# Eight tiles to a group in a fused quantised-FFN, attention and FP6 kernel: one chain of numbers per eight tiles, long stages by four

## The chip, the cores and the metric

The kernel runs on one core of a Trainium2 chip. The metric is device time in microseconds (us) of one execution, the median over runs. The compute engines are TensorE (PE, with its weight loads as PEld), VectorE (DVE), ScalarE (ACT) and GpSimd (POOL); SyncE (SP) issues all the kernel's DMAs from one queue, in order.

## The reference

`x` is [128, 64, 256] float32: 128 sequences of 64 tokens; `cond` is [128, 256]. In short, `x = x + ffn(recurrence(cond, x))`, and the output is `x + fp6_linear(block(x, cond))`. The four parts are:

1. A gated recurrence over the 64 steps, from `cond` as the first `h` and with `x` as `z`: `h = tanh(h * leak + sigmoid(h @ Wh.T + z @ Wz.T + b) * z)`.
2. A SwiGLU feed-forward (256 to 704 to 256) with int8 fake quantisation of activations and weights. The scales are maxima over the whole tensor, so `h` must be known everywhere before the down projection.
3. A hyperbolic transformer block, conditioned by `ada = t_emb @ w_ada + b_ada` (shift, scale and gate, twice). `logmap0` and `expmap0` scale every token by a function of its norm:

```
xm  = expmap0(layer_norm(logmap0(x)) * (1 + sc_msa) + sh_msa)
... attention over 64 tokens with 16 heads of 16, output projection
x   = mobius_add(x, expmap0(g_msa * logmap0(attn_out)))
xm  = expmap0(layer_norm(logmap0(x)) * (1 + sc_mlp) + sh_mlp)
ff  = plin(plin(xm, w_f1, b_f1), w_f2, b_f2)
x   = mobius_add(x, expmap0(g_mlp * logmap0(ff)))
```

4. A linear layer (256 to 256) on activations and weights rounded to an FP6 grid with a scale per 32 values.

`mobius_add(x, y)` needs, for each token, the sums x.x, y.y and x.y; everything else in it is arithmetic on these numbers. That arithmetic, and that of logmap0, expmap0 and layer_norm, is what "number chains" means below.

## The kernel before

**Up to about 310 us** the recurrence runs (PE, ACT and DVE in turn), then the first feed-forward products are made and `h` is written to DRAM (`h_d`). The change does not touch this.

**`fused`** does the rest over 64 tiles of 128 tokens. A group has GT = 4 tiles, so there are 16 groups; the work is done in pairs of tiles. Its stages:

- `front(i)`: loads `h` (`hl`, two pairs ahead) and `x` (`xr`), quantises to int8 on POOL, casts (`hq`), does the down projection on PE (`dn`), writes the block input `x1` to SBUF and to DRAM (`x1_d`), and takes mean and variance of every token (`stats`).
- `norms(k)`: `ln_coeffs`, a chain of some 22 small DVE steps with two reciprocal roots, for attention's group k + LA and mlp's group k together, with one column for each tile (2 x GT columns). Then `modulate` (scale and shift by `ada` rows, with the sum of squares `un`), `radial` (the root of `un`, `su`) and `clip_ball`.
- `attention(i)`: qkv in three passes of split float32, head norms, scores, softmax, values; then `radial` of `tn` (`full`), the output projection `wo`, the gate (POOL multiply, L737) and two sums of squares (`tail_sums`).
- `mlp(i)`: the product of both linear layers as one, `radial` of `fn2` (`cf`), gate, sums, and x.(ga) by `x_dot`.
- `tail(k)`: for the attention result it loads `x1` again from DRAM (`xt`) and takes x.(ga) by `x_dot`; then `tail_coeffs`, a chain of some 30 small DVE steps, for attention's group k and mlp's group k - LM together; then `combine` (L797, one DVE step a tile) for both, and `stats` of attention's result.
- `fp6(i)`: block maxima, scaling, rounding, transposes, the last linear layer (`fp`), the addition of `x1` read from DRAM, and the store.

The program order is a loop over k that calls tail(k), norms(k), fp6(k - LM), mlp(k), attention(k + LA), front(k + LA + 1), with LA = 5 and LM = 3. This is not the order on the engines: the framework's scheduler (`schedule_with_timeline_sim=True`) places instructions on each engine by a simulated time, and functions marked `@first` (`radial`, `ln_coeffs`, `tail_coeffs`) have a raised priority. Once built, every engine and the SP queue run their lists strictly in order. CFG holds the buffer counts of each pool tag and which engine (V, G, S) does which step.

Reciprocal roots are made by `rsqrt` in one of two ways: as a power on POOL (L640) if there are at most `len_pow` = 16 columns, otherwise by ln and exp on ACT (L643, L644) and a Newton step of three DVE instructions (L645 to L647).

Of the kernel before, what the change touches and what calls it, by code (L numbers as in the profile page):

```python
# [16 lines left out]
AF = mybir.ActivationFunctionType  # L17
# [5 lines left out]
P = 128  # L23
# [21 lines left out]
TS = 4  # L45
CFG = {'rnd': 'S', 'ef': 8, 'fill': {'x1a': 'V', 'mod0': 'V'}, 'hold': [3, 0], 'mk': 3, 'mv': 6, 'xs': 3, 'la': 3, 'sb': 7, 'qks': 'GGGG', 'deq': 'VV', 'first': 1000, 'hb': 2, 'q_h': 'P', 'q_x1': 'P', 'q_xr': 'P', 'q_ot': 'P', 'q_out': 'P', 'q_ada': 'P', 'room': [[0.3, 0.3, 0.55], [0.5, 0.4, 0.2]], 'qv': 64, 'p1': 'GVGVGVGV', 'x1': 3, 'u1': 16, 'u2': 6, 'qkv': 2, 'sq': 1, 'uT1': 2, 'uT2': 2, 'qM': 2, 'kT': 2, 'e': 4, 'oT': 1, 'yT': 1, 'hq': 2, 'hl': 2, 'xr': 1, 'ot': 2, 'ada00': 2, 'ada02': 2, 'ada10': 2, 'ada12': 4, 'dn': 1, 'qk': 2, 'sc': 2, 'ao': 1, 'ml': 1, 'fp': 1, 'mod0': 'GGGV', 'mod1': 'VVVV', 'sqm0': 'SSSS', 'sqm1': 'SSSS', 'su0': 'VVVV', 'su1': 'VGVG', 'q8': 'GGGGGG', 'hqc': 'SSSVVV', 'qm': 'SSSS', 'x1a': 'GV', 'gate0': 'GGGG', 'gate1': 'GGGG', 'yb': 'GG', 'va': 'GGGG', 'sqt': 'SSSS', 'sqg': 'SSSS', 'sqo': 'SSVS', 'f2e': 'SSSS', 'early': 0, 'q8f': 'VVVVVV', 'hqf': 'SSSVVV', 'fl': 1, 'un': 2, 'jsu': 1, 'LA': 5, 'LM': 3, 'tl': 6, 'ord': 1, 'xt': 3, 'q_xt': 'P'}
GT = 4
NGR = NTILE // GT

# [501 lines left out]
def fused(ctx, tc, a, out_tok, x_tok, L):  # L551
# [13 lines left out]
    one = ones[:, 0:1]  # L565
    len_pow = 4 * GT
    nhalf = ep.tile([P, len_pow], F32, name="nhalf", tag="nhalf", bufs=1)
# [15 lines left out]
    class Pairs:  # L583


        def __init__(self, tag):
            self.t = [big(tag, [P, 2, D]) for _ in range(GT // 2)]

# [124 lines left out]

    def modulate(src, nm, aa, which, i0, u, un):

        for g in range(GT):
            ss = load_ada(which, 0, 2, i0 + g)
            ug = u[g]
            if pick(f"mod{which}", g) == "G":
                G_.tensor_scalar(ug, src[g], nm[:, g : g + 1], aa[:, g : g + 1], ALU.add, ALU.mult)  # L720
                G_.tensor_tensor(ug, ug, ss[:, 1, :], ALU.mult)
                G_.tensor_tensor(ug, ug, ss[:, 0, :], ALU.add)
            else:
                V.scalar_tensor_tensor(ug, src[g], nm[:, g : g + 1], ss[:, 1, :], ALU.add, ALU.mult)  # L724
                V.scalar_tensor_tensor(ug, ug, aa[:, g : g + 1], ss[:, 0, :], ALU.mult, ALU.add)
            square_sum(pick(f"sqm{which}", g), f"u{which}", ug, un[:, g : g + 1])

    def clip_ball(u, su, which):

        for g in range(GT):  # L730
            scale(pick(f"su{which}", g), u[g], u[g], su[:, g : g + 1])

# [91 lines left out]

    pairs = range(GT // 2)

# [24 lines left out]

    def front(i):

        i0 = at[0] = i * GT
        x1 = x1s[i] = Pairs("x1")
        mv1 = get_mv(i - LA)[:, HA, :]
        for h2 in pairs:
            pr = i0 // 2 + h2
# [28 lines left out]

    def attention(i, u, sums):

        i0 = at[0] = i * GT  # L890
        oall = u
        tn = mk("tn", GT)
        for h2 in pairs:
            qkv = big("qkv", [P, 2, 3 * D])
# [96 lines left out]
            for g in (2 * h2, 2 * h2 + 1):  # L991
                square_sum(pick("sqo", g), "o", oall[g], tn[:, g : g + 1])
        full = radial(tn, "full", R, 1.0 / RATIO)
        av = u
        for h2 in pairs:
            pt = bank("ao")
            for i in range(2):
                for c in range(2):
                    o = (2 * i + c) * P
                    turn(pt[:, o : o + P], oall[2 * h2 + i][:, c * P : (c + 1) * P])  # L1000
            oT = big("oT", [P, 4, P])
            S.copy(oT.rearrange("p c t -> p (c t)"), pt)
            pm = bank("ao")
            for i in range(2):
                g = 2 * h2 + i
                for c in range(2):
                    PE.matmul(pm[:, i * D : (i + 1) * D], lhsT=oT[:, 2 * i + c, :], rhs=wo[:, c, :],
                              start=(c == 0), stop=(c == 1))
            for i in range(2):
                g = 2 * h2 + i  # L1010
                V.scalar_tensor_tensor(av[g], pm[:, i * D : (i + 1) * D], full[:, g : g + 1], bo,
                                       ALU.mult, ALU.add)
                gb = load_ada(0, 2, 1, i0 + g)
                tail_sums(av[g], gb[:, 0, :], sums, g, 0, "a")
        return av

    def mlp(i, u, x2, sums):

        i0 = at[0] = i * GT
        fn2 = mk("fn2", GT)  # L1020
        for h2 in pairs:
            uT = big("uT2", [P, 2, 2, 2 * P], F32R)
# [7 lines left out]
            for i in range(2):  # L1030
# [9 lines left out]
                V.tensor_tensor_reduce(out=junk3, in0=pm[:, :D], in1=u[g], scale=1.0, scalar=0.0,  # L1040
                                       op0=ALU.mult, op1=ALU.add, accum_out=fn2[:, g : g + 1])
                if pick("f2e", g) == "S":
# [4 lines left out]
        av = u  # L1047
        for g in range(GT):
            V.scalar_tensor_tensor(av[g], u[g], cf[:, g : g + 1], bf2,  # L1049
                                   ALU.mult, ALU.add)  # L1050
# [5 lines left out]
    def fp6(i, av, s2):  # L1056

        i0 = at[0] = i * GT
        sab = mk("sab", GT)
        S.activation(sab, s2, AF.Abs)  # L1060
        for h2 in pairs:
            y = av.t[h2].rearrange("p g d -> p (g d)")
# [4 lines left out]
            hh = slice(2 * h2, 2 * h2 + 2)  # L1067
            V.scalar_tensor_tensor(of(msc), of(msc), 1.0 / 7.5, bc_in(sab[:, hh], 8), ALU.mult, ALU.mult)
            V.tensor_scalar(msc, msc, 1e-30, None, ALU.max)
# [27 lines left out]
    def norms(k, xs):  # L1097

        on_a, on_m = k + LA < NGR, k >= 0
        mv = mvs.pop(k)  # L1100
        un, nm = mk("un"), mk("nm")
        if not (on_a and on_m):
            G_.memset(un, 1.0)
        x2n, la = ln_coeffs(mv, xs)
        V.tensor_scalar(nm, mv[:, :, 0], -1.0, None, ALU.mult)
        todo = []
        if on_m:
            um = ums[k] = Pairs("u2")
            todo.append((1, k, us[k], um, HM))
        if on_a:  # L1110
            ua = uas[k + LA] = Pairs("u1")
            todo.append((0, k + LA, x1s[k + LA], ua, HA))
        for which, i, x, u, h in todo:
            at[0] = i * GT
            modulate(x, nm[:, h], la[:, h], which, i * GT, u, un[:, h])
            if not CFG["jsu"]:
                clip_ball(u, radial(un[:, h], f"su{which}"), which)
        if CFG["jsu"]:
            su = radial(un, "su")
            for which, i, x, u, h in todo:  # L1120
                clip_ball(u, su[:, h], which)
        if on_a:
            G_.tensor_copy(get_tail(k + LA)[2][:, HA], x2n[:, HA])
        if on_m:
            G_.tensor_copy(get_tail(k + LM)[2][:, HM], x2n[:, HM])

    def tail(k):
# [3 lines left out]
        if on_a:  # L1131

            own = mk("xss", bufs=CFG["sb"])
            G_.memset(own, 1.0)
            x1 = Pairs("xt")
            for h2 in pairs:
                move("xt", out=x1.t[h2], in_=x1_d[:, GT * k + 2 * h2 : GT * k + 2 * h2 + 2, :])
            for g in range(GT):
                x_dot(x1[g], uas[k][g], sums(k, HA), g, "a")
        ag2, xg, x2n = tails.pop(k)  # L1140
        s_, r = tail_coeffs(ag2, xg, x2n, xss.pop(k - LM, None), own, HA, HM)
        if on_a:
            u, mv = uas.pop(k), get_mv(k)

            for g in range(GT):
                combine(u[g], x1[g], u[g], r[:, HA], g)
                stats(mv[:, HM, :][:, g, :], u[g], 2)
# [11 lines left out]
    for i in range(CFG["fl"]):  # L1159
        front(i)  # L1160
    for k in range(-LA, NGR + LM):
        done = tail(k) if k >= 0 else None
        if done and CFG["ord"] == 0:
            fp6(k - LM, *done)
        if k < NGR:
            norms(k, xss.get(k))
        if done and CFG["ord"] == 1:
            fp6(k - LM, *done)
        if 0 <= k < NGR:
            mlp(k, ums[k], us[k], sums(k + LM, HM))  # L1170
        if k + LA < NGR:
            attention(k + LA, uas[k + LA], sums(k + LA, HA))
        if done and CFG["ord"] == 2:
            fp6(k - LM, *done)
        if k + LA + CFG["fl"] < NGR:
            front(k + LA + CFG["fl"])

# [47 lines left out]
```

## Time and profile before

| | |
|---|---|
| median of 13 runs | 1382.49 us (1376.08 to 1390.08) |
| the profiled execution | 1380.64 us, span 1378.7 us |
| DVE busy | 1150.2 us, 83%, 3608 instructions |
| PE busy | 1088.3 us, 79% |
| POOL busy | 828.2 us, 60% |
| ACT busy | 813.8 us, 59% |
| mean granted TensorE clock | 0.862 |
| bytes read from HBM, written | 115.94 MB, 46.14 MB |

Busy times are from one profiled execution. Rows of the profile name the line, the engine, the operation and out<-in by the program's names; after the first bar stand the busy time in us and the mean ns of one, after the second the engine's idle time before them and what ended it. A row of the stretch view has for each engine its busy us with the count of instructions, then the mean granted TensorE clock, the DMA share and GB/s. A row of the waits view has the total us, the number of times and the longest.

### The profile page before, as it was taken

The numbers are of one execution on the slowest core, as the hardware profiler recorded it, in microseconds if no ns is written. First come the engines' busy times: TensorE is split into PE (matmuls) and PEld (weight loads), VectorE is DVE, ScalarE is ACT, GpSimd is POOL, SyncE is SP. The second block draws the span as 40 slices with busy tenths as digits, with TensorE's granted clock in tenths as the row PEclk, the third lists the DMA queues.
The fourth block names the chain that finished last, engine by engine and source line by source line (L and its number), as shares of the span: only waits on it lengthen the run. The fifth ranks groups of instructions, "written<-read, shape, count | busy, mean of one in ns | idle before, by whom it ended". The sixth has DMA issues, their size and how long they took to land. (4 is left out here: it accounts for less than half of the span.)

```text
span 1378.7 us, 23854 instructions
## 1 busy us (share of the span) xinstructions
PE 1088.3 (79%) x7364; PEld 740.7 (54%) x7380; DVE 1150.2 (83%) x3608; ACT 813.8 (59%) x2364; POOL 828.2 (60%) x1043
## 2 busy tenths in 40 slices
PE   7999967974489887898868888598987889785645
PEld 4656542332366555666646666466655666553433
DVE  5666669996888788998998879999799998889873
ACT  2545438981376756667746667555766676744341
POOL 3111208865588867787775776768667675746551
PEclk9999979995699978999858999788998899886575
DMA  7112245669724414442154441504414131314211
GB/s 235 54 54 85 70 194 194 267 256 286 225 88 124 123 49 141 136 150 68 51 172 125 131 132 44 160 26 136 139 39 138 55 112 50 104 58 121 62 47 46
DMA packets 119305, 163.65 MB, mean 119 GB/s; under 512 B 10885, under 2 KB 72074, under 8 KB 119178
## 3 DMA queue, kind: packets, MB, share of 16 engines
q1 hardware_dynamic: 119178, 162.13, 37.7%
q8 instruction: 58, 0.95, 0.3%
q14 instruction: 69, 0.57, 0.1%
HBM read 115.94 MB, written 46.14 MB: 118 GB/s over the span
## 5 line engine op out<-in xcount | busy, mean ns | idle before, releaser
L609 ACT ACTIVATE junk<-u 128x256 bf16<-128x256 f32 x432 | 183.0, 426 | 149.6 <-POOL u L737 53.8
L915 PE MATMUL qk<-wqkv,uT 128*128 128x512 f32 (+1 forms) x768 | 183.8, 377 | 15.8 <-DVE uT L906 9.5
L737 POOL TENSOR_TENSOR u<-u,ada 128x256 f32<-128x256 f32 x128 | 101.7, 797 | 101.8 <-ACT junk L609 95.0
L915 PEld LDWEIGHTS qk<-wqkv,uT 128*128 128x128 f32 x768 | 126.8, 201 | 37.2 <-DVE uT L906 13.2
L981 PE MATMUL ao<-va,e 128*64 128x34 f32 x2048 | 91.3, 246 | 62.5 <-DVE u L986 22.8
L981 PEld LDWEIGHTS ao<-va,e 128*64 128x64 f32 x2048 | 82.1, 161 | 88.9 <-issue 49.6
L966 PE MATMUL sc<-qM,kT 64*64 64x256 f32 x1024 | 122.9, 425 | 5.0 <-ACT kT L956 3.4
L1037 PE MATMUL ml<-wm,uT 128*128 128x512 f32 (+1 forms) x384 | 115.0, 437 | 0.0
L1037 PEld LDWEIGHTS ml<-wm,uT 128*128 128x128 f32 x384 | 80.3, 211 | 52.1 <-issue 22.0
L616 ACT ACTIVATE qM<-sc,mhead 128x256 f32<-128x256 f32 x256 | 102.0, 494 | 5.8 <-PE sc L92 5.7
L945 POOL TENSOR_TENSOR va<-qkv,comb 64x256 f32<-64x256 f32 x128 | 85.1, 665 | 32.2 <-PE ao L981 26.2
L880 PE MATMUL dn<-wdT,hq 128*128 128x256 bf16 (+1 forms) x384 | 67.8, 321 | 45.7 <-DVE x L882 20.6
L513 POOL TENSOR_TENSOR hv<-uv,sil 128x512 f32<-128x512 f32 x44 | 57.6, 1312 | 66.3 <-DVE am L516 48.5
L974 ACT ACTIVATE e<-sc 128x512 f32<-128x512 f32 x128 | 72.5, 599 | 28.9 <-PE ao L981 15.2
L609 ACT ACTIVATION_READ_ACCUMULATOR junk<-u 128x1 f32 x432 | 86.9, 201 | 0.0
L434 PE MATMUL pg<-hsT,WT 128*128 128x128 f32 x504 | 75.8, 290 | 9.5 <-ACT hsT L446 9.0
L1091 PE MATMUL fp<-wfT,yT 128*128 128x256 f32 x256 | 83.2, 458 | 0.0
L434 PEld LDWEIGHTS pg<-hsT,WT 128*128 128x128 f32 x504 | 65.1, 192 | 31.5 <-ACT hsT L446 28.8
L941 POOL TENSOR_TENSOR qkv<-qkv,comb 128x512 f32<-128x512 f32 x64 | 69.6, 1103 | 16.8 <-DVE comb L932 5.7
L620 POOL TENSOR_SCALAR hb<-hl,cu 128x1280 int8<-128x1280 f32 x64 | 62.9, 988 | 26.8 <-DMA hl<-h_d 11.5
L966 PEld LDWEIGHTS sc<-qM,kT 64*64 64x64 f32 x1024 | 54.7, 143 | 43.1 <-issue 10.2
L880 PEld LDWEIGHTS <-hq 128*128 128x128 bf16 (+1 forms) x384 | 38.1, 110 | 72.5 <-issue 33.7
(285 smaller groups left out, 3162.6 us busy)
## 6 DMA issues: line engine op xcount, KB each, us to landing
ada<-ada_d SPq DMA_DIRECT2D x128, 256.0 KB, 3.6
h_d<-hv SPq DMA_DIRECT2D x80, 256.0 KB, 2.1
hl<-h_d SPq DMA_DIRECT2D x32, 640.0 KB, 5.9
ada<-ada_d SPq DMA_DIRECT2D x128, 128.0 KB, 2.5
xt<-in_xT_dram SPq DMA_DIRECT2D x16, 512.0 KB, 4.7
xr<-in_x_dram SPq DMA_DIRECT2D x32, 256.0 KB, 3.8
x_d<-x SPq DMA_DIRECT2D x32, 256.0 KB, 2.3
xt<-x_d SPq DMA_DIRECT2D x32, 256.0 KB, 2.9
```

The source lines that it names most:

```text
L434: lp = PE.matmul(pg[c][:, st], lhsT=WT[:, k, c * P : (c + 1) * P], rhs=hp[:, k, :], start=False, stop=False, skip_group_check=True)
L609: S.activation(junk, src, AF.Square, accum_out=acc)
L616: S.activation(dst, src, AF.Copy, scale=by)
L737: ENG[pick(f"gate{which}", g)].tensor_tensor(av, av, gb, ALU.mult)
L880: PE.matmul(py[:, i * D : (i + 1) * D], lhsT=hq[r, j, i * P : (i + 1) * P], rhs=wdT[r, j, :], start=(i == 0 and j == 0), stop=(j == 5), sk ...
L915: PE.matmul(pm[:, :n_], lhsT=uT[:, z, k, cs], rhs=wqkv[:, w, k, lo:hi], start=False, stop=(k == 1 and q == 2))
L945: ENG[pick("va", g)].tensor_tensor(va[r, :, s, 0:HD], qkv[r, xy, 512:768].rearrange("p (h d) -> p h d", d=HD), bc_in(comb[r, xy * 48 + 32 ...
L966: PE.matmul(sc[rr][s * T : (s + 1) * T, c * 256 : (c + 1) * 256].rearrange("p (v t) -> p v t", v=4), lhsT=kTs[xy][r, c, s * T : (s + 1) * ...
L974: S.activation(e.rearrange("p c v t -> p (c v t)"), sc[rr], AF.Exp, scale=1.0 / math.sqrt(HD))
L981: PE.matmul(pv[xy * T : (xy + 1) * T, hh], lhsT=E[2 * xy + hh // 4][:, c, hh % 4, :], rhs=vas[(2 * h2 + xy) % 4][:, c * 8 + hh], start=Tru ...
L1037: PE.matmul(pm[:, cs], lhsT=uT[:, z, k, i * P : (i + 1) * P], rhs=wm[:, w, k, cs], start=False, stop=(k == 1 and q == 2))
L1091: PE.matmul(o, lhsT=yT[:, 2 * i + c, :], rhs=wfT[:, c, :], start=False, stop=(c == 1))
```

## The change

A group has GT = 8 tiles (8 groups), and SUB = 4. `ln_coeffs` and `tail_coeffs` run once for eight tiles of each of their two users. modulate, clip_ball, attention, mlp, fp6 and front take an argument `sub` and do four tiles at a time: `norms` is a generator that yields between the halves, and the main loop lets the stages take turns by halves. Buffers of `Pairs` are taken pair by pair as they are first written, not all at once. The attention's x.(ga) moves from `tail` to the end of `attention`, where `x1` is loaded for it (`xd`); `tail` loads `x1` again (`xt`) where it combines. `len_pow` stays 16 columns (2 x GT), so the 32 columns of `tail_coeffs` now go by ACT and DVE. LA and LM are 2 groups each. Buffer counts change: x1 3 to 5, u2 6 to 8, xt 3 to 2, xd 2 (new), uT2 2 to 1, hq 2 to 1, ada12 4 to 2, mk 3 to 2, sb 7 to 5, tl 6 to 5 (LM 3 to 2, LA 5 to 2).

```diff
-GT = 4
+GT = 8
+SUB = 4
...
-    len_pow = 4 * GT
+    len_pow = 2 * GT
...
-            self.t = [big(tag, [P, 2, D]) for _ in range(GT // 2)]
+            self.tag, self.t = tag, {}
+
+        def take(self, h2):
+            t = self.t[h2] = big(self.tag, [P, 2, D])
+            return t
...
-    def modulate(src, nm, aa, which, i0, u, un):
+    def modulate(src, nm, aa, which, i0, u, un, sub):
...
+        for g in tiles(sub):
+            if g % 2 == 0:
+                u.take(g // 2)
...
-        for h2 in pairs:
+        for h2 in pairs(sub):
+            xd = big("xd", [P, 2, D])
+            move("xt", out=xd, in_=x1_d[:, i0 + 2 * h2 : i0 + 2 * h2 + 2, :])
             pt = bank("ao")
...
                 tail_sums(av[g], gb[:, 0, :], sums, g, 0, "a")
+                x_dot(xd[:, i, :], av[g], sums, g, "a")
...
+        for sub in parts:
+            yield
+            un = mk("un", 2 * SUB)
...
+            for which, i, x, u, h, c in todo:
+                at[0] = i * GT
+                modulate(x, nm[:, h], la[:, h], which, i * GT, u, un[:, c], sub)
+            su = radial(un, "su")
+            for which, i, x, u, h, c in todo:
+                clip_ball(u, su[:, c], which, sub)
...
             x1 = Pairs("xt")
-            for h2 in pairs:
-                move("xt", out=x1.t[h2], in_=x1_d[:, GT * k + 2 * h2 : GT * k + 2 * h2 + 2, :])
-            for g in range(GT):
-                x_dot(x1[g], uas[k][g], sums(k, HA), g, "a")
...
             for g in range(GT):
+                if g % 2 == 0:
+                    move("xt", out=x1.take(g // 2), in_=x1_d[:, GT * k + g : GT * k + g + 2, :])
                 combine(u[g], x1[g], u[g], r[:, HA], g)
...
+        steps = norms(k, xss.get(k)) if k < NGR else iter(())
+        next(steps, None)
+        for sub in parts:
+            next(steps, None)
+            if done:
+                fp6(k - LM, *done, sub)
+            if 0 <= k < NGR:
+                mlp(k, ums[k], us[k], sums(k + LM, HM), sub)
+            if k + LA < NGR:
+                attention(k + LA, uas[k + LA], sums(k + LA, HA), sub)
+            if k + LA + CFG["fl"] < NGR:
+                front(k + LA + CFG["fl"], sub)
```

More of the change, by code (lines that the diff above doesn't have):

```diff
@@ L45 @@
 TS = 4
-CFG = {'rnd': 'S', 'ef': 8, 'fill': {'x1a': 'V', 'mod0': 'V'}, 'hold': [3, 0], 'mk': 3, 'mv': 6, 'xs': 3, 'la': 3, 'sb': 7, 'qks': 'GGGG', 'deq': 'VV', 'first': 1000, 'hb': 2, 'q_h': 'P', 'q_x1': 'P', 'q_xr': 'P', 'q_ot': 'P', 'q_out': 'P', 'q_ada': 'P', 'room': [[0.3, 0.3, 0.55], [0.5, 0.4, 0.2]], 'qv': 64, 'p1': 'GVGVGVGV', 'x1': 3, 'u1': 16, 'u2': 6, 'qkv': 2, 'sq': 1, 'uT1': 2, 'uT2': 2, 'qM': 2, 'kT': 2, 'e': 4, 'oT': 1, 'yT': 1, 'hq': 2, 'hl': 2, 'xr': 1, 'ot': 2, 'ada00': 2, 'ada02': 2, 'ada10': 2, 'ada12': 4, 'dn': 1, 'qk': 2, 'sc': 2, 'ao': 1, 'ml': 1, 'fp': 1, 'mod0': 'GGGV', 'mod1': 'VVVV', 'sqm0': 'SSSS', 'sqm1': 'SSSS', 'su0': 'VVVV', 'su1': 'VGVG', 'q8': 'GGGGGG', 'hqc': 'SSSVVV', 'qm': 'SSSS', 'x1a': 'GV', 'gate0': 'GGGG', 'gate1': 'GGGG', 'yb': 'GG', 'va': 'GGGG', 'sqt': 'SSSS', 'sqg': 'SSSS', 'sqo': 'SSVS', 'f2e': 'SSSS', 'early': 0, 'q8f': 'VVVVVV', 'hqf': 'SSSVVV', 'fl': 1, 'un': 2, 'jsu': 1, 'LA': 5, 'LM': 3, 'tl': 6, 'ord': 1, 'xt': 3, 'q_xt': 'P'}
-GT = 4
+CFG = {'rnd': 'S', 'ef': 8, 'fill': {'x1a': 'V', 'mod0': 'V'}, 'hold': [3, 0], 'mk': 2, 'mv': 6, 'xs': 3, 'la': 3, 'sb': 5, 'qks': 'GGGG', 'deq': 'VV', 'first': 1000, 'hb': 2, 'q_h': 'P', 'q_x1': 'P', 'q_xr': 'P', 'q_ot': 'P', 'q_out': 'P', 'q_ada': 'P', 'room': [[0.3, 0.3, 0.55], [0.5, 0.4, 0.2]], 'qv': 64, 'p1': 'GVGVGVGV', 'x1': 5, 'u1': 16, 'u2': 8, 'qkv': 2, 'sq': 1, 'uT1': 2, 'uT2': 1, 'qM': 2, 'kT': 2, 'e': 4, 'oT': 1, 'yT': 1, 'hq': 1, 'hl': 2, 'xr': 1, 'ot': 2, 'ada00': 2, 'ada02': 2, 'ada10': 2, 'ada12': 2, 'dn': 1, 'qk': 2, 'sc': 2, 'ao': 1, 'ml': 1, 'fp': 1, 'mod0': 'GGGV', 'mod1': 'VVVV', 'sqm0': 'SSSS', 'sqm1': 'SSSS', 'su0': 'VVVV', 'su1': 'VGVG', 'q8': 'GGGGGG', 'hqc': 'SSSVVV', 'qm': 'SSSS', 'x1a': 'GV', 'gate0': 'GGGG', 'gate1': 'GGGG', 'yb': 'GG', 'va': 'GGGG', 'sqt': 'SSSS', 'sqg': 'SSSS', 'sqo': 'SSVS', 'f2e': 'SSSS', 'early': 0, 'q8f': 'VVVVVV', 'hqf': 'SSSVVV', 'fl': 1, 'un': 2, 'jsu': 1, 'LA': 2, 'LM': 2, 'tl': 5, 'ord': 1, 'xt': 2, 'q_xt': 'P', 'xd': 2}
+GT = 8
+SUB = 4
 NGR = NTILE // GT
@@ L725, in modulate, with clip_ball @@
                 V.scalar_tensor_tensor(ug, ug, aa[:, g : g + 1], ss[:, 0, :], ALU.mult, ALU.add)
[L726 to L731, printed above, removed]
+            c = g % SUB
+            square_sum(pick(f"sqm{which}", g), f"u{which}", ug, un[:, c : c + 1])
+    def clip_ball(u, su, which, sub):
+        for g in tiles(sub):
+            c = g % SUB
+            scale(pick(f"su{which}", g), u[g], u[g], su[:, c : c + 1])
     def tail_sums(av, gb, sums, g, which, tag):
@@ L823, in runs, with tiles, pairs @@
         yield es[5], half, slice(5, 6)
-    pairs = range(GT // 2)
+    parts = range(GT // SUB)
+    def tiles(sub):
+        return range(sub * SUB, (sub + 1) * SUB)
+    def pairs(sub):
+        return range(sub * SUB // 2, (sub + 1) * SUB // 2)
     HA, HM = slice(0, GT), slice(GT, 2 * GT)
@@ L850, in sums, with front @@
         return ag2[:, h], ag2[:, 2 * GT + h.start : 2 * GT + h.stop], xg[:, h]
-    def front(i):
+    def front(i, sub):
         i0 = at[0] = i * GT
-        x1 = x1s[i] = Pairs("x1")
+        if sub == 0:
+            x1s[i] = Pairs("x1")
+        x1 = x1s[i]
         mv1 = get_mv(i - LA)[:, HA, :]
-        for h2 in pairs:
+        for h2 in pairs(sub):
+            x1.take(h2)
             pr = i0 // 2 + h2
@@ L886, in front, with attention @@
             move("x1", out=x1_d[:, i0 + 2 * h2 : i0 + 2 * h2 + 2, :], in_=x1.t[h2])
-    def attention(i, u, sums):
+    def attention(i, u, sums, sub):
         i0 = at[0] = i * GT
         oall = u
-        tn = mk("tn", GT)
-        for h2 in pairs:
+        tn = mk("tn", SUB)
+        for h2 in pairs(sub):
             qkv = big("qkv", [P, 2, 3 * D])
@@ L991, in attention @@
             for g in (2 * h2, 2 * h2 + 1):
-                square_sum(pick("sqo", g), "o", oall[g], tn[:, g : g + 1])
+                square_sum(pick("sqo", g), "o", oall[g], tn[:, g % SUB : g % SUB + 1])
         full = radial(tn, "full", R, 1.0 / RATIO)
         av = u
-        for h2 in pairs:
+        for h2 in pairs(sub):
+            xd = big("xd", [P, 2, D])
+            move("xt", out=xd, in_=x1_d[:, i0 + 2 * h2 : i0 + 2 * h2 + 2, :])
             pt = bank("ao")
@@ L1010, in attention @@
                 g = 2 * h2 + i
-                V.scalar_tensor_tensor(av[g], pm[:, i * D : (i + 1) * D], full[:, g : g + 1], bo,
+                V.scalar_tensor_tensor(av[g], pm[:, i * D : (i + 1) * D], full[:, g % SUB : g % SUB + 1], bo,
                                        ALU.mult, ALU.add)
@@ L1014, in attention, with mlp @@
                 tail_sums(av[g], gb[:, 0, :], sums, g, 0, "a")
+                x_dot(xd[:, i, :], av[g], sums, g, "a")
         return av
-    def mlp(i, u, x2, sums):
+    def mlp(i, u, x2, sums, sub):
         i0 = at[0] = i * GT
-        fn2 = mk("fn2", GT)
-        for h2 in pairs:
+        fn2 = mk("fn2", SUB)
+        for h2 in pairs(sub):
             uT = big("uT2", [P, 2, 2, 2 * P], F32R)
@@ L1040, in mlp @@
                 V.tensor_tensor_reduce(out=junk3, in0=pm[:, :D], in1=u[g], scale=1.0, scalar=0.0,
-                                       op0=ALU.mult, op1=ALU.add, accum_out=fn2[:, g : g + 1])
+                                       op0=ALU.mult, op1=ALU.add, accum_out=fn2[:, g % SUB : g % SUB + 1])
                 if pick("f2e", g) == "S":
@@ L1047, in mlp @@
         av = u
-        for g in range(GT):
-            V.scalar_tensor_tensor(av[g], u[g], cf[:, g : g + 1], bf2,
+        for g in tiles(sub):
+            V.scalar_tensor_tensor(av[g], u[g], cf[:, g % SUB : g % SUB + 1], bf2,
                                    ALU.mult, ALU.add)
@@ L1054, in mlp, with fp6 @@
         return av
-    def fp6(i, av, s2):
+    def fp6(i, av, s2, sub):
         i0 = at[0] = i * GT
-        sab = mk("sab", GT)
-        S.activation(sab, s2, AF.Abs)
-        for h2 in pairs:
+        sab = mk("sab", SUB)
+        S.activation(sab, s2[:, sub * SUB : (sub + 1) * SUB], AF.Abs)
+        for h2 in pairs(sub):
             y = av.t[h2].rearrange("p g d -> p (g d)")
@@ L1067, in fp6 @@
             hh = slice(2 * h2, 2 * h2 + 2)
-            V.scalar_tensor_tensor(of(msc), of(msc), 1.0 / 7.5, bc_in(sab[:, hh], 8), ALU.mult, ALU.mult)
+            V.scalar_tensor_tensor(of(msc), of(msc), 1.0 / 7.5, bc_in(sab[:, h2 * 2 % SUB : h2 * 2 % SUB + 2], 8),
+                                   ALU.mult, ALU.mult)
             V.tensor_scalar(msc, msc, 1e-30, None, ALU.max)
@@ L1100, in norms @@
         mv = mvs.pop(k)
-        un, nm = mk("un"), mk("nm")
-        if not (on_a and on_m):
-            G_.memset(un, 1.0)
+        nm = mk("nm")
         x2n, la = ln_coeffs(mv, xs)
         V.tensor_scalar(nm, mv[:, :, 0], -1.0, None, ALU.mult)
[L1106 to L1121, printed above, removed]
         if on_a:
@@ L1125, in norms @@
             G_.tensor_copy(get_tail(k + LM)[2][:, HM], x2n[:, HM])
+        todo = []
+        if on_m:
+            um = ums[k] = Pairs("u2")
+            todo.append((1, k, us[k], um, HM, slice(SUB, 2 * SUB)))
+        if on_a:
+            ua = uas[k + LA] = Pairs("u1")
+            todo.append((0, k + LA, x1s[k + LA], ua, HA, slice(0, SUB)))
+        for sub in parts:
+            yield
+            un = mk("un", 2 * SUB)
+            if not (on_a and on_m):
+                G_.memset(un, 1.0)
+            for which, i, x, u, h, c in todo:
[4 more added lines that the diff above has]
+                clip_ball(u, su[:, c], which, sub)
+        yield
     def tail(k):
@@ L1135, in tail @@
             x1 = Pairs("xt")
-            for h2 in pairs:
-                move("xt", out=x1.t[h2], in_=x1_d[:, GT * k + 2 * h2 : GT * k + 2 * h2 + 2, :])
-            for g in range(GT):
-                x_dot(x1[g], uas[k][g], sums(k, HA), g, "a")
         ag2, xg, x2n = tails.pop(k)
@@ L1159, in fused @@
     for i in range(CFG["fl"]):
-        front(i)
+        for sub in parts:
+            front(i, sub)
     for k in range(-LA, NGR + LM):
         done = tail(k) if k >= 0 else None
[L1163 to L1176, printed above, removed]
+        steps = norms(k, xss.get(k)) if k < NGR else iter(())
+        next(steps, None)
+        for sub in parts:
+            next(steps, None)
[7 more added lines that the diff above has]
+                front(k + LA + CFG["fl"], sub)
 _INS = {
```

## The prediction

> **What bounds the kernel now.** I read the page's engine sums first, then a cut of the span into four stretches, then the waits of VectorE (DVE), TensorE (PE) and the SyncE queue, then the rows of the number chains.
>
> ```profile
> span 1378.7 us, 23854 instructions
> PE 1088.3 (79%) x7364; PEld 740.7 (54%) x7380; DVE 1150.2 (83%) x3608; ACT 813.8 (59%) x2364; POOL 828.2 (60%) x1043
> ```
>
> DVE is the fullest engine, but over a span in which the recurrence and the first projection (to 312 us) are not touched. So I cut at 312 (end of the untouched part), 564 (first mlp matmul, row L1037) and 1234 (last attention work):
>
> ```profile
> core 0: us, PE busy (x) PEld busy (x) DVE busy (x) ACT busy (x) POOL busy (x), PEclk, DMA share, GB/s
> 312.00:564.00 252.00, 188.41 (x1468) 129.27 (x1470) 201.90 (x609) 144.00 (x397) 182.17 (x241) 0.79 0.51 149
> 564.00:1234.00 670.00, 552.92 (x4383) 406.58 (x4389) 611.15 (x2029) 441.19 (x1361) 465.99 (x591) 0.89 0.33 100
> 1234.00:1378.70 144.70, 81.52 (x286) 58.64 (x284) 105.48 (x405) 49.18 (x160) 65.65 (x79) 0.65 0.23 71
> ```
>
> In the 670 us where attention and mlp run together DVE is busy 91.2%, PE 82.5%, nothing else over 70%. In that stretch the waits of PE end on DVE (ao on u L986 20.0 us, on u L1011 16.4, ml on uT L1029 12.6), and DVE itself waits for any one thing 9.5 us at most. DVE sets the pace there. The last 145 us are a mix of chains and fp6 work with no full engine.
>
> ```profile
> L640 POOL TENSOR_TENSOR r<-q,nhalf 128x16 f32<-128x16 f32 x19 | 56.2, 2959 | 21.8 <-DVE xg L776 6.8 <-DVE q L753 6.3 <-DVE msc L1068 4.9
> L682 DVE TENSOR_SCALAR nln<-nln 128x8 f32<-128x8 f32 x21 | 9.2, 436 | 0.3
> L763 DVE TENSOR_TENSOR zztc<-nntc 128x8 f32<-128x8 f32 x19 | 5.4, 284 | 0.3
> ```
>
> These are three of some fifty rows of the number chains: 8 or 16 numbers per partition, and yet 0.2 to 0.4 us each on DVE. The 22 or so of ln_coeffs (pln rows of L624/L625, L666 to L698, L1105) add up to 123.9 us over 21 runs, 5.90 us a run; the 30 of tail_coeffs (pptc rows, L753 to L793) to 125.3 us over 19 runs, 6.59 us a run. Together 249.2 us of DVE's 1150.2; 158.6 of it (64%) starts between 564 and 1234 us.
>
> **Part 1: half as many chains.** With eight tiles in a group ln_coeffs runs 10 times instead of 21, tail_coeffs 10 instead of 19. By the order of the built programs DVE has 479 fewer instructions (509 chain steps gone, 30 new).
> - Removed by mean rows: 11 x 5.90 + 9 x 6.59 = 124.2 us.
> - Added: tail_coeffs takes the root of 32 numbers, over the limit of 16, so the POOL power becomes two ACT and three DVE steps (L643 to L647), 10 times. The same three on 128x102 take 0.32 + 0.43 + 0.34 = 1.09 us; three of the smallest steps 0.48. So 5 to 11 us, I take 7 (32 columns are nearer to 16).
> - Wider steps: the 16-wide L753 takes 207 ns, the 8-wide L758 198: 9 ns x 50 x 10 = 4.5 us.
> - Net by mean rows 124 - 7 - 4.5 = 113 us.
>
> The mean is not the step's own price. Matching each 8-wide step of the trace with what POOL did meanwhile: 332 of 992 had no POOL work beside them and took 161 ns; 151 took over 260 ns, 103.5 us in all, and lay beside POOL's long tensor steps (L941, L945, L620, L737, L1072; the powers of L640 cover 1.0 us of it). Those POOL steps stay. By the 161 ns alone the removal is 509 x 0.161 = 82, net 70 us. So 70 to 113; I take the middle, about 90, because a stall that met a removed step will only sometimes find another DVE step in its place. The Trainium skill (SBUF — State Buffer, Who interferes with whom) speaks for the low end: DVE and GpSimd share one pair of ports as an exclusive lock, held for the whole instruction by who issued first. By that rule the stalls belong to the POOL steps and pass to the next DVE step that needs the pair, and the sum is 70.
>
> POOL loses 56.2 us of r powers and, at 16 columns by the 2.92 us median of that row, 20 x 2.92 = 58.4 instead of 73.1 for rnln and lnaln: about 73 us with one su fewer. POOL was 70% busy in the paced stretch, so I count that at nothing; DVE's own work covers it. If POOL were the next limit, it would be worth at most the 73.
>
> What it is worth: 64% of 70 to 113 is 45 to 72 us of DVE in the paced stretch, at 91.2% busy 49 to 79 us of time. What is late next is PE: 552.9 us of matmuls must still fit. The fullest 100 us of the trace (900 to 1000) has PE at 88.9%; 552.9 / 0.889 = 622, which leaves 48 us. I take that lower number, **-48**.
>
> **Part 2: the start.** Chains need eight tiles of front before the first one. In the built PE order 108 down-projection matmuls stand ahead of the first qkv one, where 84 did (4 tiles more). Before, those 84 ran from 310.8 us to 363.0, at up to 1.04 DMA share: 3.7 us a tile, so +15 us. Against it: the first mlp matmul stands behind 16 tiles of qkv instead of 20 (L915's 183.8 us and L912's 41.6, over 64 tiles, are 3.5 us of PE each: -14), and 2 ln runs in place of 5 save 3 x 5.9 = 18 us of DVE, of which half on the path (DVE is 80% busy here): -9. Sum **-8**, bounds -30 to +15.
>
> **Part 3: the end.** In both orders the last attention work stands at the same place, with 12 tiles of mlp to go; behind it the new order has 24 tiles of fp6, the old 20. The last two additions into ot start 6.6 us apart (1368.17 and 1374.79 in the chain that ended last), so two pairs more cost +13. Fewer chains (32.5 us of DVE in that stretch, nearly halved) give -14 if all lie on the path. **-1**, bounds -15 to +15.
>
> **Part 4: the dots and the loads.** The 64 x.(ga) dots (412 ns median) move from tail to attention's end: same count, same DVE time; each waits for the gate multiply of POOL, as the square beside it did. Nothing. New are 32 loads xd of 256 KB: at the 2.9 us and by the DMA share of 0.33 in the paced stretch, hidden two buffers ahead; without that cover 2.9 us a pair, 93 us at most. tail's xt loads now stand four in a row in SP's queue on two buffers, where two stood on three: the third waits for the first combine, and all queued behind it (ada, hl, xr, xd) waits too. Taken at nothing, because DVE waited for the ada loads only 20.9 us in all while SP stood blocked far longer:
>
> ```profile
> SPq L575 <- POOL u L737: 190.3, 74, 16.9
> SPq L575 <- DVE u L797: 94.2, 24, 18.7
> DVE u L724 <- DMA ada<-ada_d: 20.9, 19, 4.0
> ```
>
> The lone uT2 buffer costs nothing: the single ml bank already makes a pair wait for the one before. The single hq buffer lets the casts wait for the down projection (2.2 us of DVE's waits with two): 0 to 10 us.
>
> **Sum**: 1380.6 (this execution; its span 1378.7) - 48 - 8 - 1 = 1323.6. The median of the runs is 1.9 above this execution, so I forecast 1325.
>
> **The rivals.**
> 1. *PE does not close up* (chance 0.15). Chains halve, but the new PE order is lumpier: all four o pairs of a group and all four fp6 pairs stand together, between stretches of mlp and qkv. PE's clock is 0.89 in the paced stretch and 0.5 at the start; more idle lumps cost clock. For: PE already waits for single DVE steps up to 8.6 us. Against: DVE's steps are finely mixed in the new order, chain steps between attention and mlp steps. Half the gain: 1380.6 - 28 + 1.9, about 1354.
> 2. *Slower: the loads on few buffers* (0.19). xt has two buffers for four pairs and the ada12 gates two instead of four. Each of 8 tails would wait two landings of 2.9 us (46 us), each of 16 mlp halves two of 2.5 (80 us), in DVE's and POOL's own order, with the SP queue held behind them. Full price 126 against the 57 won; it decides once over 45% of it is exposed. At two thirds: 1382.5 - 57 + 84, about 1409. For: SP is blocked 94 us on L797 even now. Against: those blocks hardly reach DVE, and the new DVE order has attention and mlp steps between the second and the third combine.
> 3. *The ends eat it* (0.06): start +15, end +15, low DVE price and a PE that stays at 85%: within 0.3% of before, about 1382.
>
> **How the numbers follow.** The forecast has 0.60, with its own range 1276 (79 from the paced stretch, 30 less by start and end, minus 2) to 1362 (20 won). The range that leaves out 2 in 10 reaches into rival 2: 1274 to 1400. Four us either way (0.3%) is about what a measurement of this kernel can tell from no change. Faster 0.60 + 0.14 + 0.01 = 0.75, same 0.04, slower 0.21.
>
> **What would show it.** Right: some 3130 DVE instructions and 1040 to 1080 us busy; POOL near 755; no r power row, L645 to L647 on 128x32 x10; PE at 88% or more in the stretch where both stages run; the first qkv matmul near 378 us; DVE waiting for xt and ada under 40 us. Wrong: DVE below 85% there with PE no fuller (rival 1), or combine L797 and the gates L737 waiting for DMA by tens of us (rival 2), or a drain well over 160 us.

## The result, and the profile after

The changed kernel takes 1458.08 us (median of 11 runs, 1452.02 to 1465.62), against 1384.5 us for the kernel before in the same comparison: 1.053 times as long, 95% interval 1.051 to 1.056. The profiled execution spans 1455.0 us. I had forecast 1325.

The page of the changed kernel opens with the same two lines as that of before:

```profile
span 1455.0 us, 23388 instructions
PE 1132.5 (78%) x7365; PEld 762.9 (52%) x7380; DVE 1075.2 (74%) x3129; ACT 815.0 (56%) x2345; POOL 750.5 (52%) x952
```

The work went as planned: 479 DVE instructions and 75.0 us of DVE fewer, 77.7 us of POOL fewer. The time went up all the same. The stretch view, cut at the first mlp matmul (566 us) and the end of the attention (1295), says where; columns as before:

```profile
312.00:566.00 254.00, 186.01 (x1383) 123.23 (x1386) 160.36 (x458) 128.91 (x352) 151.76 (x194) 0.73 0.50 149
566.00:1295.00 729.00, 601.91 (x4443) 435.48 (x4447) 579.73 (x1736) 456.67 (x1387) 435.11 (x563) 0.85 0.35 103
1295.00:1455.00 160.00, 79.16 (x310) 57.98 (x309) 103.72 (x369) 50.39 (x161) 49.33 (x61) 0.74 0.20 63
```

Up to the first mlp matmul little changes (254 us, 252 before). The paced stretch is 59 us longer (729, 670 before), the end 15 us (160, 145). In the paced stretch DVE fell from 91.2% to 79.5% busy and PE did not fill the gap: 82.6%, as before (82.5%), and part of that is the lower granted clock (0.85, 0.89 before). No engine is nearly full there any more, so something makes all of them wait.

The qkv matmuls alone (the stretch view for line L933, the L915 of before; only PE has any), around one group, show the shape of it:

```profile
core 0: us, PE busy (x) PEld busy (x), PEclk, DMA share, GB/s
818.00:860.00 42.00, 18.48 (x84) 12.70 (x84) 1.00 0.31 92
860.00:936.00 76.00, 2.58 (x12) 1.92 (x12) 0.82 0.45 128
936.00:996.00 60.00, 21.91 (x96) 15.85 (x96) 0.97 0.19 55
```

One group's 96 matmuls end by 878 us, the next group's start at 936. In between the chains run. The chain that leads to the group after that (the critical chain within the window from 930 to 1075 us: start, us, what) reads:

```profile
971.14 0.74 POOL u L746
...
975.00 0.35 DVE q L762
...
987.21 1.19 DVE u L806 x3
...
1013.89 1.71 PE fp L1113 x4
...
1023.61 0.19 DVE tln L698
...
1045.99 4.64 DMA ada<-ada_d
...
1068.81 1.66 POOL sur L645
...
1073.03 1.33 DVE u L623 x3
```

The last attention gate of a group (L746, the L737 of before) lets tail_coeffs start (q, 975 us); then come combine (L806), the fp6 work between, ln_coeffs (tln), an `ada` load, the root `sur`, and only then the clips (L623, 1073 us): 98 us from q to these clips. They are those of the second half of the group that starts next; the clips of its first half came at 1056 us and its first qkv matmul at 1063, 88 us after q.

I measured this for every group, from the start and end times in the traces. In the changed kernel tail's first step follows attention's last output step by 3.5 to 12.8 us (mean 7.7); before, by 4.8 to 51.2 (mean 22). From tail's first step to the first qkv matmul of the attention LA groups later pass 61 to 112 us (mean 90), and the attention of one group takes 137 us from first qkv to last output. By construction the three add up to LA periods: (137 + 8 + 90) / 2 is 118 us for eight tiles. The sum proves nothing; that tail now follows the end of attention with so little slack suggested the theory.

**Theory (loop).** `norms(k)` computes ln_coeffs and su jointly for mlp's group k and attention's group k + LA. So attention(k + 2) waits for tail(k), which waits for attention(k). Two groups share this loop (16 tiles); before, five did (20 tiles). **Rivals:** the two groups of u2 that fp6 must give back (release); the few buffers, the extra loads and the SP queue (loads; rival 2 of the prediction); lumps of eight tiles as such (width; close to rival 1).

### The profile page after: what moved, and what is told of

Read it like the earlier page. It is cut to its first block, busy times and chain, and to the rows that moved or that the text cites. A ratio compares the mean times of both kernels' runs of the same rounds, so it can differ in the third digit from the quotient of the medians.

```text
span 1455.0 us, 23388 instructions
## 1 busy us (share of the span) xinstructions
PE 1132.5 (78%) x7365; PEld 762.9 (52%) x7380; DVE 1075.2 (74%) x3129; ACT 815.0 (56%) x2345; POOL 750.5 (52%) x952
## 5 line engine op out<-in xcount | busy, mean ns | idle before, releaser
L933 PE MATMUL qk<-wqkv,uT 128*128 128x512 f32 (+1 forms) x768 | 183.0, 378 | 14.5 <-ACT uT L923 10.3
L746 POOL TENSOR_TENSOR u<-u,ada 128x256 f32<-128x256 f32 x128 | 98.9, 776 | 127.7 <-ACT junk L614 105.9
L984 PE MATMUL sc<-qM,kT 64*64 64x256 f32 x1024 | 146.0, 449 | 20.0 <-ACT kT L974 14.7
L933 PEld LDWEIGHTS qk<-wqkv,uT 128*128 128x128 f32 x768 | 127.8, 202 | 38.8 <-ACT uT L923 13.8
L999 PE MATMUL ao<-va,e 128*64 128x34 f32 x2048 | 97.7, 249 | 51.5 <-DVE u L1004 27.6
L999 PEld LDWEIGHTS ao<-va,e 128*64 128x64 f32 x2048 | 86.3, 164 | 83.1 <-issue 53.9
L898 PE MATMUL dn<-wdT,hq 128*128 128x256 bf16 (+1 forms) x384 | 75.7, 352 | 48.8 <-DVE x L900 16.1
L984 PEld LDWEIGHTS sc<-qM,kT 64*64 64x64 f32 x1024 | 63.7, 152 | 67.7 <-ACT kT L974 23.4
L938 DVE TENSOR_REDUCE nh<-sq 128x48 f32<-128x768 f32 x64 | 60.4, 944 | 40.9 <-ACT sq L937 40.8
L992 ACT ACTIVATE e<-sc 128x512 f32<-128x512 f32 x128 | 76.5, 611 | 24.8 <-PE sc L984 17.0
L1027 PE MATMUL ao<-wo,oT 128*128 128x256 f32 x256 | 74.6, 443 | 10.4 <-ACT oT L1022 10.2
```

Of the source, the lines that this page charges most:

```text
L746: ENG[pick(f"gate{which}", g)].tensor_tensor(av, av, gb, ALU.mult)
L898: PE.matmul(py[:, i * D : (i + 1) * D], lhsT=hq[r, j, i * P : (i + 1) * P], rhs=wdT[r, j, :], start=(i == 0 and j == 0), stop=(j == 5), sk ...
L933: PE.matmul(pm[:, :n_], lhsT=uT[:, z, k, cs], rhs=wqkv[:, w, k, lo:hi], start=False, stop=(k == 1 and q == 2))
L984: PE.matmul(sc[rr][s * T : (s + 1) * T, c * 256 : (c + 1) * 256].rearrange("p (v t) -> p v t", v=4), lhsT=kTs[xy][r, c, s * T : (s + 1) * ...
L992: S.activation(e.rearrange("p c v t -> p (c v t)"), sc[rr], AF.Exp, scale=1.0 / math.sqrt(HD))
L999: PE.matmul(pv[xy * T : (xy + 1) * T, hh], lhsT=E[2 * xy + hh // 4][:, c, hh % 4, :], rhs=vas[(2 * h2 + xy) % 4][:, c * 8 + hh], start=Tru ...
```

## The experiments

**Same buffers, groups of four (a_g4).** The changed code with its buffers, loads and moved x.(ga), but chains four tiles wide and as many tiles in flight.

```diff
-GT = 8
+GT = 4
-... 'LA': 2, 'LM': 2, 'sb': 5, 'tl': 5
+... 'LA': 4, 'LM': 4, 'sb': 8, 'tl': 7
-    len_pow = 2 * GT
+    len_pow = 4 * GT
```

> The changed kernel's code and buffer counts (x1 5, u1 16, u2 8, xt 2, xd 2, uT2 1, hq 1, ada12 2, mk 2), but with GT = 4 and one part, LA = 4 and LM = 4: as many tiles in flight as with two groups of eight, chains 4 tiles wide as before; sb 8, tl 7, the POOL power for up to 16 columns as before. Loop: four groups share a loop of some 150 us, 38 us for four tiles, under what the engines need (about 48): 1380 to 1405 us, as before the change. Release: u2 holds four groups, as deep as before: also about 1385. Loads: the same buffers and the same 32 more loads, so 1440 us or more.

Measured: 1396.93 us, 1.008 (1.004 to 1.011) of before. The buffers, the 32 new loads, the moved dots and the new leads (LA 4 instead of 5, LM 4 instead of 3) together cost 12 us; the single terms could offset each other. Rival 2, which asked for 1440 us or more here, falls: the rest of the loss, 61 us, comes with GT = 8 and what goes with it (two groups in flight, the 32-column root on ACT and DVE).

**The chains of attention and mlp apart (a_split).** ln_coeffs, su and tail_coeffs take one side at a time, eight tiles wide, attention's side first; groups, LA, LM and big buffers stay (mv, sb and tl have four buffers).

```diff
-        x2n, la = ln_coeffs(mv, xs)
+        x2n, la = ln_coeffs(mv, xss.get(i) if w == "m" else None, w)
...
-            su = radial(un, "su")
+            clip_ball(u, radial(un, f"su{w}"), which, sub)
...
-        s_, r = tail_coeffs(ag2, xg, x2n, xss.pop(k - LM, None), own, HA, HM)
+        s_, r = tail_coeffs(ag2, xg, x2n, None, "a")
...
+        s_, r = tail_coeffs(ag2, xg, x2n, xss.pop(k), "m")
```

> The changed kernel with the number chains of attention and of mlp apart: ln_coeffs, the su root and tail_coeffs run for eight tiles of attention or of mlp alone (16 + 16 runs of 8 columns instead of 10 + 10 of 16, roots of 8 and 16 columns as POOL powers). Groups of eight, LA = 2, LM = 2, all buffers of the big tiles as in the changed kernel. attention(k+2) now needs no tail(k): its u1 slots come free when mlp(k-2) is combined. DVE busy rises from 1075 to about 1140 us. Theory (loop): the loop attention(k), tail(k), norms(k), attention(k+2) is cut, so 1380 to 1415 us in spite of more DVE work. Rival (width): lumps of eight tiles starve PE whatever waits for what: 1450 to 1520. Rival (release of u2 by fp6): attention gets free, mlp still waits: 1410 to 1450.

Measured: 1392.95 us, 1.007 (1.004 to 1.009) of before. DVE busy is 1114.9 us, 40 more than in the changed kernel, and the time is 65 us less. The loss goes when the loop is cut, with the width, the buffers and u2 unchanged. That speaks against width as the main cause, and mlp's own wait for u2 slots is not it either; whether that wait costs time through attention, by the joint su, is the question of the next run.

**Only su apart (a_su2).** The root of un for each side, attention first; ln_coeffs and tail_coeffs stay joint.

```diff
-            for which, i, x, u, h, c in todo:
+            for which, i, x, u, h, c in todo[::-1]:
...
-                modulate(x, nm[:, h], la[:, h], which, i * GT, u, un[:, c], sub)
-            su = radial(un, "su")
...
+                un = mk(f"un{which}", SUB)
+                modulate(x, nm[:, h], la[:, h], which, i * GT, u, un, sub)
+                clip_ball(u, radial(un, f"su{which}"), which, sub)
```

> The changed kernel with the su root (radial of un) taken for attention and for mlp apart, attention first; ln_coeffs and tail_coeffs stay joint; mv 5 buffers instead of 6 for room. Attention's clips no longer wait for mlp's modulate, which waits for u2 slots that fp6 gives back. Loop: the way from tail to attention's clips (116 us in the trace of the changed kernel) gets 15 to 30 us shorter, half of it a group: 1395 to 1445 us. Width: within 10 us of the changed kernel, 1450 to 1468. Release: the larger part of the loss goes, 1390 to 1420.

Measured: 1438.63 us, 1.040 (1.036 to 1.045). Within the loop's range, and short of the 1390 to 1420 that release asked for; some 20 us of the loss lie in this joint alone. But the reason given did not come: from tail's first step to the first qkv of two groups later pass 91 us in the mean (90 in the changed kernel). What got shorter is attention itself, 129 us from first qkv to last output instead of 137.

**ln and su apart, tail joint (a_lnsplit).**

```diff
-        s_, r = tail_coeffs(ag2, xg, x2n, None, "a")
+        s_, r = tail_coeffs(ag2, xg, x2n, xss.pop(k - LM, None), own, HA, HM)
```

(against a_split, for both sides again)

> The changed kernel with ln_coeffs and the su root apart for attention and mlp, as in a_split, but tail_coeffs joint as in the changed kernel (10 runs). It tells which of the two joints closes the loop. If the joint ln and su do: attention(k+2) is free of tail(k) but for its u1 slots, 1380 to 1410 us, with some 35 us less DVE work than a_split. If the u1 slots do, which come free in the joint tail's combine of mlp's tiles and so after attention(k): 1425 to 1450, near a_su2. Width: 1450 or more.

Measured: 1377.01 us, 0.994 (0.991 to 0.997) of before, 3 us under the first range. So the joint ln and su carry the loss (81 us against the changed kernel), and the joint tail does not: joining it again saves 16 us against a_split. The loop is not gone in this kernel, it is shorter. u1 holds four groups, and in its trace the modulate of attention's groups 4 to 7 starts 1 to 3 us after tail has begun to combine mlp's tiles, which frees their slots. From tail's first step to the first qkv of two groups later pass 55 to 61 us there (61 to 112 in the changed kernel), and groups 2 and 3 do not wait for a tail at all. The stretch view of this kernel, to be read against 566 to 1295 above:

```profile
566.00:1240.00 674.00, 555.67 (x4390) 410.58 (x4395) 572.08 (x1818) 449.71 (x1398) 421.97 (x563) 0.89 0.34 102
1240.00:1376.00 136.00, 74.46 (x272) 53.31 (x271) 86.15 (x302) 42.21 (x131) 39.65 (x50) 0.70 0.22 68
```

Nearly all the matmuls that the changed kernel does in 729 us (4443) are done in 674 (4390), at the old clock of 0.89.

**The same at groups of four (a_lnsplit_g4)**: the two edits together (GT = 4, LA = LM = 4; ln and su apart).

> a_lnsplit at GT = 4, LA = 4 and LM = 4 (as many tiles in flight, same big buffers; sb 8, tl 7, POOL powers up to 16 columns): 32 ln runs and 20 tails, each 4 tiles wide, instead of 16 and 10. It shows what the wider chains are worth once the loop does not bind. By the prediction's prices DVE has 16 x 5.9 + 10 x 6.6 - 7 = 150 us more work by mean rows, about 100 by 161 ns a step, so 1190 to 1240 us busy. If DVE's work sets the time: 1430 to 1480 us. If the width is worth little: 1375 to 1400.

Measured: 1362.36 us, 0.984 (0.978 to 0.990) of before: the fastest of all, and faster than both kernels. My expectation from DVE's work (1430 to 1480) was far off; even its alternative (1375 to 1400) was too high, as was the DVE time expected (1190 to 1240). Its page and its paced stretch:

```profile
span 1360.8 us, 24213 instructions
PE 1082.6 (80%) x7365; PEld 737.2 (54%) x7380; DVE 1171.6 (86%) x3845; ACT 813.0 (60%) x2387; POOL 833.6 (61%) x1086
564.00:1200.00 636.00, 541.93 (x4386) 400.19 (x4388) 601.80 (x2112) 443.88 (x1394) 460.21 (x612) 0.92 0.34 104
```

DVE does 80 us more than at GT = 8 (1171.6, 1091.7), at 94.6% busy in the stretch, and the kernel is still 15 us faster. So saved DVE work did not become time even where the loop is shorter.

**The kernel before with less lead (b_la3, b_la2)**: `'LA': 5` to 3, and to 2, nothing else.

> The kernel before with LA = 3 instead of 5, nothing else (groups of four, 12 tiles of attention ahead). Loop: a latency of about 150 us is shared by three groups, 50 us for four tiles, about what the engines need (47): 1385 to 1440 us. Width: nothing in it depends on LA as long as other work is ready: within 15 us of before.

> The kernel before with LA = 2, nothing else (8 tiles of attention ahead). Loop: 75 us for four tiles instead of 47, over some 13 groups: 1650 to 1800 us. Width: within 30 us of before.

Measured: 1463.24 us, 1.059 (1.055 to 1.063), and 1586.92 us, 1.147 (1.142 to 1.152). The direction is the loop's and rules out that LA does not matter; the sizes were off both ways. I had taken a fixed latency of 150 us; in these traces attention of a group takes 100 and 77 us in the mean, and the way from tail to the qkv that waits for it 75 and 61 (141 and 104 before): the latency shrinks when less is in flight.

**The mlp side ahead in the program (a_split_m)**, against a_split: the order of the calls for the two sides is swapped in `norms` and in the main loop.

> a_split with the mlp side put ahead in the program (tail of attention, norms of mlp, then norms of attention). In a_split the first mlp matmul came at 597 us instead of 564 before the change, while the stretch from there to the end of attention was shorter (637 instead of 670). Loop: the chains are as free as in a_split, so only the start moves: 1365 to 1395 us. Width: no change against a_split, 1385 to 1400.

Measured: 1395.35 us, 1.009 (1.006 to 1.013). No gain, as the second expectation had it, and the first mlp matmul at 598.5 us instead of 596.9: the order of the calls is not what delays it. Nor is it the order of the two sides, which a_split had swapped along with the split, that won its 65 us.

**A miss: room for more buffers.** This came before the splits. To try LA = 3 and a third group of u2 I made room by sharing the tiles that take unread results, by single xd and hb buffers and by single temporaries.

```diff
-        junk = pl.tile([P, D], BF16, name="junk", tag=f"junk{tag}{e}", bufs=1)
+        junk = pl.tile([P, D], BF16, name="junk", tag=f"junk{e}", bufs=1)
...
-        junk = pl.tile([P, D], BF16, name="junk", tag=f"junkx{tag}", bufs=1)
+        junk = pl.tile([P, D], BF16, name="junk", tag="junkV", bufs=1)
...
-        k = lambda name: mk(f"{name}tc")
+        k = lambda name: mk(f"{name}tc", bufs=1)
... 'xd': 2 -> 1, 'hb': 2 -> 1, 'mv': 6 -> 4
```

> The changed kernel with some 8 KB of SBUF per partition freed: the junk outputs of one engine share one tile, xd and hb have one buffer instead of two, the temporaries of tail_coeffs one instead of two. It is the base for the next two. Theory (loop): attention(k+2) starts from norms(k), norms(k) waits for tail(k), tail(k) waits for attention(k); with LA = 2 the period of a group of eight is half of that loop's latency (clips at 930 and 1165 us in the trace: 235 us for two groups). Loop: 1455 to 1475 us. Rival (release): u2 holds two groups, so mlp's modulate waits for fp6 of two groups before, and the joint su makes attention wait too: 1455 to 1475. Rival (loads): few buffers and the SP queue: 1460 to 1490, since xd has one buffer.

> The trimmed kernel with LA = 3 instead of 2, and u1 20 pairs instead of 16, nothing else. Loop: the same latency is shared by three groups, 80 us a group, under what the engines need (about 100), so the stretch with both stages falls from 729 us by 50 to 90 us; total 1370 to 1410 us. Release: still two groups of u2, no gain, within 15 us of the trimmed kernel. Loads: no gain, within 15 us.

> The trimmed kernel with u2 12 pairs (three groups) instead of 8, LA stays 2. Loop: the chain from tail to norms no longer waits for fp6, so the loop may be some 10 to 20 us shorter: 0 to 40 us less than the trimmed kernel. Release: the cause is gone, 50 us or more less than the trimmed kernel. Loads: within 15 us.

Measured: 1898.27 us for the base, 1958.65 with LA = 3, 1887.94 with u2 of three groups. The base itself lost 440 us, in a regime of its own, so neither of the other two says anything of the loop; LA = 3 at eight tiles stays untried on the changed kernel itself. One part of the trim alone told which part it was:

> The changed kernel with only one part of the trim: the unread junk outputs of squares and dots share one tile on ACT and one on DVE, instead of nine tiles. If sharing a tile forces the engines to take the stages in program order, it carries the trim's whole loss: 1850 to 1900 us. If the single xd and hb buffers did it: within 20 us of the changed kernel, 1440 to 1480.

Measured: 1871.41 us (one run). Sharing the unread tiles carries nearly all of it. Among PE's waits the mlp transposes stand first, behind the clips of DVE (179.3 us, 12.3 in the changed kernel):

```profile
POOL u L746 <- ACT junk L614: 185.1, 89, 4.6
PE ml L93 <- DVE u L623: 179.3, 16, 15.7
DVE junk L752 <- POOL u L746: 136.4, 83, 5.4
```

In the built PE order the stage changes 428 times instead of 594 (runs of neighbouring matmuls into qk, sc, ao, ml, fp or dn). I take it that a tile shared by two stages ties them to the order of the program, so that the scheduler can no longer mix them; that the tie is the cause was not tried on its own.

## Why the prediction was wrong

**The step that failed is "What it is worth" in Part 1, with "What is late next is PE" behind it.** The sum took DVE's share (91.2%) as the pace and turned each saved microsecond of DVE into time, capped by PE at 88.9%. I asked which engine would be full next, not which wait would be last next. LA falls from five groups to two in the change, and norms joins mlp's group k with attention's group k + LA. Both stand in the code, and I listed neither as a cost; Part 2 even booked the shorter lead (16 tiles of qkv ahead of the first mlp instead of 20) as 14 us won. I had seen that chain steps stand between attention and mlp steps in DVE's order and took this for cover. It was cover for DVE, but the qkv matmuls of the next group waited behind the whole chain.

What the runs showed in its place: with ln and su joint, attention's group k + 2 waits for the whole way through tail(k) and norms(k), 90 us in the mean; with both apart 81 us of time come back (1458.08 to 1377.01) though DVE does 16 us more. And DVE's work was not the pace without this wait either: 80 us less of it went with 15 us more time (a_lnsplit against a_lnsplit_g4).

By its parts:

- **Part 1, the work**: right. 3129 DVE instructions (3130), 1075.2 us busy (1040 to 1080), POOL 750.5 (755). The saving of 75.0 us lies near the low end of 70 that the 161 ns a step gave, not at the 90 I took; that the low end came out is luck. The chain rows fell from 249.2 to 145.5 us in sum, 103.7 less (113 by mean rows), the other DVE rows by 11.6. What the prediction missed is that neighbouring DVE steps overlap in the trace: all rows add up to 1368.6 us before, in which DVE was busy for 1150.2, and to 1253.2 in 1075.2 after. So 249.2 "of DVE's 1150.2" set a sum of rows against busy time, and 40 us of the removed rows had lain over a neighbour. The nln step has the same mean as before (436 ns) at twice the width:

```profile
L687 DVE TENSOR_SCALAR nln<-nln 128x16 f32<-128x16 f32 x10 | 4.4, 436 | 0.2
L650 DVE TENSOR_TENSOR rs<-r 128x32 f32<-128x32 f32 x10 | 3.3, 327 | 1.9 <-ACT r L649 1.9
```

  Half of its ten runs took 157 to 206 ns, half 483 to 1062. The Trainium skill (SBUF — State Buffer, Who interferes with whom) states that the port pair of DVE and GpSimd is an exclusive lock, held for a whole instruction; the prediction drew from it that all stalls would pass to other DVE steps. These rows do not show that: 85 of 500 chain steps of 16 columns took over 260 ns, 59.9 us in all, where it had been 151 of 992 and 103.5 us, and the other rows did not grow.
- **Part 1, its worth**: wrong, -48 forecast, +59 measured. Nor does the width pay where the loop is shorter. From first to last mlp matmul a_lnsplit takes 723 us (599 to 1322 in its trace) and a_lnsplit_g4 755 (567 to 1322), but that is the later start: at 599 us a_lnsplit has 25 tiles of qkv, 16 of output projection and none of mlp behind it, a_lnsplit_g4 22, 12 and 4. At 900 us they stand nearly level (45 and 44 tiles of qkv, 36 and 36, 25 and 25; fp6 16 and 12), and the last mlp matmul comes at 1322 us in both, though a_lnsplit_g4 has 60 us more DVE work between 599 and 1322. What the two-group loop that is left takes from a_lnsplit was not separated.
- **Part 2, the start**: -8 forecast, +2 measured (first mlp matmul at 566 us; the first qkv at 375, forecast 378, 363 before). So the +15 for four more tiles of front measured +12, and the two gains, 23 together, 10. a_lnsplit starts its first mlp matmul 32 us later than a_lnsplit_g4; that is not the width alone: the changed kernel, as wide, starts at 566, while its next attention group waits.
- **Part 3, the end**: -1 forecast, +15 measured. From the last mlp matmul to the end of the span it is 47 us before and after, so the 15 us lie ahead of that, between the last attention work and the last mlp matmul (97 and 113); no run tells how much of it is the fp6 work (+13 in the sum) and how much the chains (-14 in the sum). a_lnsplit and a_lnsplit_g4 differ behind the last mlp matmul, by 14 us (53 and 39), with eight tiles of fp6 to go in both: in a_lnsplit all eight wait for the last combine (1339 us on), in a_lnsplit_g4 four of them have theirs at 1314.
- **Part 4**: nothing forecast; 12 us by a_g4, together with its leads. The combines did not wait for xt in any row that counts (0.3 us), but the waits for ada grew, over the 40 us that the prediction had set as a sign (20.9 and 15.4 before):

```profile
DVE u L731 <- DMA ada<-ada_d: 49.8, 34, 7.5
POOL u L728 <- DMA ada<-ada_d: 31.4, 14, 4.8
```

- **The rivals**: rival 2 had the right sign by a wrong mechanism (a_g4). Rival 1 named the symptom, a PE that does not close up and a lower clock, and its sign came (DVE at 79.5% with PE no fuller), but it gave half the gain, and its lumps are not the main cause: a_lnsplit has groups as wide and a clock of 0.89 in its stretch. In rival 3 the end of +15 came, as a part of the loss. The lower end of the forecast's own range does not add up (1382.5 - 79 - 30 - 2 is 1271.5, not 1276); nothing hangs on it.

What stays open: why joining the tail again gains 16 us over a_split (23 us of DVE work go with it, 1114.9 to 1091.7, but a_lnsplit and a_lnsplit_g4 show that less DVE work need not be less time); what delays the first mlp matmul to 597 us and later where the chains are apart at eight tiles; and what part of the small loss of a_g4 against before is the lead (LA 4 instead of 5), what part the buffers. That the joint costs at four tiles too is shown: 1396.93 against 1362.36.

## What to carry to other kernels

When a change coarsens the units of a software pipeline, write down each loop through which a unit waits for an earlier one, and how many units share it, before adding up engine time: that an engine is 91% busy does not show that its work is the pace. A chain that serves two stages at once saves instructions and ties the stages together; here undoing one such tie was worth 81 us at eight tiles and 35 us at four, while 80 us less DVE work in wider chains was worth nothing. And before a step's mean time is used as its price, compare the sum of the engine's rows with its busy time: where steps overlap, a removed row is not all time saved. When an engine does less and the time goes up, look for the engine that waits for a whole stage, line by line, not for the fullest one.

## What the runs showed that I had not expected

- More DVE work in less time: 1171.6 us busy in a span of 1360.8 (a_lnsplit_g4) against 1075.2 in 1455.0 (the changed kernel).
- The granted clock differs for nearly the same matmuls: 0.85 in the paced stretch of the changed kernel, 0.92 in that of a_lnsplit_g4 (4443 and 4386 matmuls).
- Sharing tiles that nobody reads took the kernel from 1458.08 to 1871.41 us (one run).
